# One PSUM ring, a paired fc2, and a new interleave of chunk and head in a spectral-network kernel

## The chip, the core and the metric

The kernel runs on one core of one Trainium2 chip. The metric is the device time of one launch in microseconds. Its engines are TensorE (PE, whose weight loads are the row PEld), VectorE (DVE), ScalarE (ACT), GpSimd (POOL) and SyncE (SP); POOL and SP do little else here than issue DMAs. Every engine works its own instructions in order and waits for the others by semaphores.

## The reference, cut to what matters

The input x is (8, 8, 256, 256), 8 images of 8 channels in 4 groups. Layer 0 is a Fourier network on the normalised x, added to x; layer 1 adds to that a 3x3 dilation (max) of its own normalised value.

```python
h = gconv1x1(concat([xg, grid]), fc0_w, fc0_b)      # 4 groups, width 10 each
for i in range(4):
    h = spectral_conv(h, sp_w1[i], sp_w2[i]) + gconv1x1(h, w_w[i], w_b[i])
    if i < 3:
        h = gswish(h, betas[i])
h = gswish(gconv1x1(h, fc1_w, fc1_b), betas[3])     # 128 hidden units per group
x = x + gconv1x1(h, fc2_w, fc2_b)                   # 2 channels per group
x = x + dilate3x3(group_norm(x))
```

`spectral_conv` keeps 24 x 12 modes of the 2-D Fourier transform, mixes the 10 channels of a group there with complex weights, and transforms back.

## The kernel before, in words

**Layers.** The state of one image lies in SBUF as `h`, 11 chunks of [128, 4, 512]. A layer begins with four stages that have no chunk loop. `spectrum_h` (L304 to L324) transposes and transforms along the rows, `mix` (L344 to L370) multiplies the modes with the weights `sw`: six pairs of a product and a sum of 800 elements on VectorE, then one fold on TensorE (L362) and copies into `fz`. `rows_of` (L380, L385, L395) goes back along the rows into `zt`. In the first layer `spectrum_x` takes the place of `spectrum_h`. Then `layer` goes over 11 chunks. For chunk c, `burst` (L432 or L435, then L438) makes two PSUM pairs `p_z`, and ScalarE (L444) writes `silu` of them into `h`; in the last layer VectorE (L446) and ScalarE (L448) write one pair each, and the chunk is stored to DRAM (`stored`, L450). `turn` (L407, copied by VectorE at L410) transposes the new chunk into a slot of `turned`, and `transform` (L420, copied at L421 into `zt`) makes the first transform of the next layer. The last layer has neither.

**Head.** fc1, its swish, and fc2 of an image form the *head*: 128 steps. `first(n)` makes four matmuls of 32 x 512 (L521), two groups into each of two PSUM pairs, and ScalarE (L524) writes `act` in two instructions of 128 x 1024. `second(n)` makes four matmuls (L537) from `act`. Sixteen steps accumulate into one PSUM tile `p_fc2`; then VectorE adds bias and x (L541), takes statistics (L542), and POOL stores the rows (L544). The head reads its state from DRAM, 1 MB per 12 steps into one of two tiles `hs` (L508, POOL's queue).

**Dilation.** `dilate` goes over 8 row blocks of an image: a DMA into `yin` (L561, POOL), six larger VectorE instructions (L572 to L586), and a DMA out (L587).

**Order.** PE, DVE and ACT keep the order in which the program issues (`manual_schedule`); POOL's and SP's DMAs are placed by the scheduler. The head of image b runs among the layers of image b + 1: each stage of the layers yields a cost (`CHUNK` = 1.25 for a chunk, 1 to 3 for other pieces), and 128 steps are spread over the sum of the costs. So image 0's layers run without a head, and image 7's head runs alone. Each step also advances the dilation of the image before by one of its 35 pieces. `unit` delays the second half of a unit (`second` of a step, `turn` of a chunk) behind the first half of the next one. So a chunk of the first three layers with one step stands on TensorE as: transform(c-2), burst(c), second(n-1), first(n), turn(c), transform(c-1), and so on.

**PSUM.** Eight banks: three pairs of the kind `z` (two banks each, used in rotation by `p_z`, `p_t`, `p_fc` of first and others), and two single banks `a` (`p_d`, `p_fc2` and others). A tile of a kind is given again when all its readers are done, in rotation; the first matmul into it waits for that.

```python
def ps_z(name):
    return ps.tile([128, 2, 512], F32, tag="z", bufs=3, name=name)
def ps_a(name):
    return ps.tile([128, 512], F32, tag="a", bufs=2, name=name)
```

Of the kernel before, what the change touches and what calls it, by code (L numbers as in the profile page):

```python
# [2 lines left out]

# [1 line left out]

# [16 lines left out]
G = 4  # L22
# [15 lines left out]
PIX = 2 * HW  # L38
DR = 2
STEPS = 128  # L40
CHUNK = 1.25


@with_exitstack
def fno_dilate_kernel(ctx: ExitStack, tc: tile.TileContext, a: dict, out: bass.AP):
# [6 lines left out]
    ps = ctx.enter_context(tc.tile_pool(name="ps", bufs=2, space=PSUM))  # L52
    dram = ctx.enter_context(tc.tile_pool(name="dram", bufs=2, space=bass.MemoryType.DRAM))

    def ps_z(name):
        return ps.tile([128, 2, 512], F32, tag="z", bufs=3, name=name)

    def ps_a(name):
        return ps.tile([128, 512], F32, tag="a", bufs=2, name=name)

    def part(i):
        return slice(32 * i, 32 * i + 32)
# [34 lines left out]
    h = const.tile([128, NCH, NQ, PIX], F32, tag="h", name="h")  # L97
    for c in range(NCH):
        nc.gpsimd.memset(h[:, c], 0.0)
    turned = const.tile([128, 4, 2048], F32, tag="turned", name="turned")  # L100
    yin = const.tile([128, DR + 2, HW + 2], F32, tag="yin", name="yin")
    nc.gpsimd.memset(yin, -BIG)
    y_rows = [dram.tile([C * HW + 2, HW], F32, tag=f"y{i}", bufs=1, name=f"y_rows{i}") for i in range(2)]
# [90 lines left out]
        out_["mr"] = mr  # L194

    late = [None]  # L200

    def unit(burst, after):
        burst()
        if late[0] is not None:
            late[0]()
        late[0] = after

    def flush():
        if late[0] is not None:
            late[0]()  # L210
        late[0] = None


    def spectrum_x(b, out_):

        x = turned[:, 0:2]
# [12 lines left out]
            nc.vector.tensor_scalar(x[:, i], x[:, i], mr[:, 0:1], mr[:, 1:2], ALU.subtract, ALU.mult)  # L229
        yield 1  # L230
        xt = turned[:, 2].rearrange("p (f r c) -> p f r c", f=2, r=8)
        a0 = turned[:, 3].rearrange("p (c r) -> p c r", c=128)
        for half in range(2):
            xn = x[:, half].rearrange("p (r w) -> p r w", r=8)
            for r in range(0, 8, 4):
# [101 lines left out]
    def mix(b, l, out_):  # L337

        s = [sb.tile([128, 3, G, 2, WID], F32, tag=f"S{i}", bufs=1, name=f"S{i}_{b}_{l}") for i in range(2)]
        bt, sw = out_["bt"], out_["sw"]  # L340
        for k in range(3):
            for k2 in range(2):
                pr = turned[:, 2 + k2, :800].rearrange("p (g m i) -> p g m i", g=G, i=WID)
                nc.vector.tensor_tensor(  # L344
                    pr, sw[k], bt[:, k2, k].unsqueeze(2).to_broadcast([128, G, 2 * WID, WID]), ALU.mult)
                nc.vector.tensor_reduce(  # L346
                    s[k2][:, k].rearrange("p g s o -> p (g s o)"),
                    pr.rearrange("p g m i -> p (g m) i"), AX.X, ALU.add,
                )
            if k == 0:  # L350
                sw.append(load_sw(l, 2))
            yield 3
        f = sb.tile([128, 2, 3, G, WID], F32, tag="F", bufs=1, name=f"F_{b}_{l}")
        nc.vector.tensor_tensor(f[:, 0], s[0][:, :, :, 0, :], s[1][:, :, :, 1, :], ALU.subtract)
        nc.vector.tensor_tensor(f[:, 1], s[0][:, :, :, 1, :], s[1][:, :, :, 0, :], ALU.add)
        yield 1

        p = ps_a(f"p_f_{b}_{l}")
        for slot in range(2):
            for n, (table, part_of) in enumerate(((0, slot), (1 + slot, 1 - slot))):  # L360
                for q in range(4):
                    mm(p[part(q), 120 * slot : 120 * slot + 120], fold[part(q), table, :],  # L362
                       f[part(q), part_of].rearrange("p k g o -> p (k g o)"), start=n == 0, stop=n == 1)
        nc.vector.tensor_copy(fz[0:32, :, :, 24], cz[:, l])
        if l < 2:
            nc.vector.tensor_copy(fz[0:32, :, :, 25], cz[:, 4 if l == 0 else 3])
        for q in range(4):
            dst = fz[part(q), :, :, 6 * q : 6 * q + 6].rearrange("p o g k -> p k g o")
            src = p[part(q), :240].rearrange("p (k g o) -> p k g o", g=G, o=WID)
            nc.vector.tensor_copy(dst, src)  # L370
        yield 2
# [27 lines left out]
    def layer(b, l, out_, stored, side):  # L399
        group_in_f = l % 2 == 1  # L400

        def turn(c):

            for v in range(2):
                t = ps_z(f"p_t_{b}_{l}_{c}_{v}")
                for i in range(8):
                    nc.tensor.transpose(  # L407
                        t[:, i // 4, 128 * (i % 4) : 128 * (i % 4 + 1)],
                        h[:, c, i // 2, 256 * (i % 2) + 128 * v : 256 * (i % 2) + 128 * (v + 1)], ident)
                nc.vector.tensor_copy(  # L410
                    turned[:, c % 4, 1024 * v : 1024 * (v + 1)], t.rearrange("p u w -> p (u w)"))

        def transform(c):

            t = turned[:, c % 4].rearrange("p (v f s q i) -> p v q f s i", v=2, q=NQ, f=NQ, s=2)
            p = ps_a(f"p_d_{b}_{l}_{c}")
            for v in range(2):
                for g in range(G):
# [30 lines left out]
            if l == 3:  # L449
                nc.sync.dma_start(stored[c], h[:, c].rearrange("p f w -> p (f w)"))  # L450

        def after(c):
            if l < 3:
                turn(c)

        def read_x(c):
            for g in range(G):
                nc.sync.dma_start(
# [6 lines left out]
        if l == 0:  # L465
            for c in range(NCH):
                read_x(c)
            norm_x(0)
            norm_x(1)
        for c in range(NCH):  # L470
            if l == 0 and c + 2 < NCH:
                norm_x(c + 2)
            if l < 3 and c > 1:
                transform(c - 2)
            unit(partial(burst, c), partial(after, c))
            next(side, None)
            yield CHUNK
        if l < 3:
            out_["sw"] = [load_sw(l + 1, 0), load_sw(l + 1, 1)]
            yield 1  # L480
            if late[0] is not None and late[0].func is after:
                flush()
            transform(NCH - 2)
            yield 2
            transform(NCH - 1)
# [8 lines left out]
    def layers(b, stored, d, then):  # L494


        for l in range(4):
            if l > 0:
                yield from spectrum_h(b, l, d)
# [3 lines left out]
        yield from then  # L503


    def load_state(b, c, stored):
        t = sb.tile([128, NQ, PIX], F32, tag="hs", name=f"hs_{b}_{c}")
        nc.gpsimd.dma_start(t.rearrange("p f w -> p (f w)"), stored[c])  # L508
        return t

    def head(b, stored, stats):
        hs = {0: load_state(b, 0, stored)}
        box = {}

        def first(n):

            c, blk, j = n // 12, n % 12 // 4, n % 4
            act = sb.tile([128, G, 512], F32, tag="act", name=f"act_{b}_{n}")
            pair = [ps_z(f"p_fc1_{b}_{n}_{i}") for i in range(2)]
            for g in range(G):  # L520
                mm(pair[g // 2][:, g % 2, :], w1[part(g), blk, :], hs[c][part(g), j, :],  # L521
                   start=True, stop=True)
            for i in range(2):
                nc.scalar.activation(act[:, 2 * i : 2 * i + 2, :], pair[i], AF.Silu)  # L524
            box[n] = act

        def second(n):

            t, rb = n // 16, n % 16
            if rb == 0:  # L530
                box["acc"] = ps_a(f"p_fc2_{b}_{t}")
                box["y"] = sb.tile([128, 512], F32, tag="yp", name=f"y_{b}_{t}")
                nc.gpsimd.dma_start(
                    box["y"], a["x"][b].rearrange("c (p t f) -> (c p) t f", p=16, t=8)[:, t])
            act, acc = box.pop(n), box["acc"]
            for g in range(G):
                mm(acc[part(g), :], w2[:, g, 15 - rb : 47 - rb], act[:, g, :],  # L537
                   start=rb == 0, stop=rb == 15)
            if rb == 15:
                y = box["y"]  # L540
                nc.vector.scalar_tensor_tensor(y, acc, b2, y, ALU.add, ALU.add)  # L541
                nc.vector.bn_stats(stats[:, t, :], y)  # L542
                whole = y_rows[b % 2][:]
                nc.gpsimd.dma_start(  # L544
                    bass.AP(whole.tensor, whole.offset + (1 + 2 * t) * HW, [[16 * HW, 128], [1, 512]]), y)

        for n in range(STEPS):
            if n % 12 == 0 and n // 12 + 1 < NCH:
                hs[n // 12 + 1] = load_state(b, n // 12 + 1, stored)
            unit(partial(first, n), partial(second, n))  # L550
            yield


    def dilate(b, stats):
# [33 lines left out]
            yield  # L588


    heads, tails = [], []

    def step():

# [2 lines left out]
        b, gen = heads[0]  # L597
        if next(gen, b) is b:
            heads.pop(0)
            flush()  # L600
            tails.append(dilate(b, stats_of.pop(b)))
            return step()
        if tails and next(tails[0], tails) is tails:
            tails.pop(0)
        return True

    stats_of = {}
    share, total = 0.0, None
    with tc.manual_schedule(engines={PE, DVE, ACT}):
        d = {}  # L610
        for _ in start(0, d):
            pass
        for b in range(n_img):
            stored = [dram.tile([128, NQ * PIX], F32, tag=f"hs{c}", name=f"stored_{b}_{c}") for c in range(NCH)]
            count, ahead = 0, {}
            for n in layers(b, stored, d, start(b + 1, ahead)):
                count += n
                if total is not None:
                    share += n * STEPS / total
                    while share >= 1.0:  # L620
                        share -= 1.0
                        step()
            total = total or count
            d = ahead
            if late[0] is not None and late[0].func.__name__ == "after":
                flush()
            stats_of[b] = sb.tile([128, 8, 6], F32, tag="bn_y", name=f"bn_y{b}")
            heads.append((b, head(b, stored, stats_of[b])))
        while step():
# [11 lines left out]
def _row_of():  # L641

    rows = np.full((NBLK, NQ, NCH, 2), -1)
    for n in range(HW // 2):
        c, blk, j = n // 12, n % 12 // 4, n % 4
        rows[blk, j, c] = 16 * (n % 16) + 2 * (n // 16) + np.arange(2)
    return rows

# [133 lines left out]
```

## Time and profile before

| | us |
|---|---|
| three runs | 4831.79, 4833.0, 4838.88 (median 4833.0) |
| profiled execution, its own time | 4834.64 |
| its span | 4832.9 |
| mean granted TensorE clock | 0.967 |
| PE busy | 4460.5 (92%) |
| ACT busy | 2640.7 (55%) |
| DVE busy | 2324.6 (48%) |
| POOL busy | 230.1 (5%) |
| DMA | 350.61 MB, 73 GB/s |

The profiled execution lies 1.6 us above the median of the runs, and its span 1.7 us below its own time. Busy time is the union of an engine's instructions. On TensorE several small matmuls run side by side in different rows or columns of the array, and their ends are modelled, so a busy PE can still be waiting: the distance between the starts of two groups of matmuls tells more. The bracket at the end of a line of the timeline gives the idle time before it and what ended that.

### The profile page before, as it was taken

What the parts mean: (1) busy time and instruction counts of PE and PEld (TensorE: products, weight loads), DVE (VectorE), ACT (ScalarE), POOL (GpSimd) and SP (SyncE); (2) the same over time, 40 slices, a digit from 0 to 9 for tenths busy, and PEclk for the clock granted to TensorE, in tenths of its full rate; (3) what the DMA queues carried; (4) which work ended last, traced back from release to release, by engine and by line L of the source; (5) the groups of instructions that cost most, each with busy time, mean ns of one, the idle gap of its engine ahead of it and who ended that gap; (6) DMA issues with size and microseconds to landing.
All of it is one profiled execution on the core that took longest, in us unless ns stands there. A gap on an engine that the chain in (4) does not pass through costs nothing.

```text
span 4832.9 us, 114725 instructions
## 1 busy us (share of the span) xinstructions
PE 4460.5 (92%) x52314; PEld 1956.3 (40%) x52314; DVE 2324.6 (48%) x3195; ACT 2640.7 (55%) x2717; POOL 230.1 (5%) x365
## 2 busy tenths in 40 slices
PE   4776999999999999999999999999899999999991
PEld 2443444434443444434444344433444344443220
DVE  6556443457434664446544474345643465442303
ACT  1221565655555656565555655565555565656881
POOL 2000000001000000000000000000100000000100
PEclk8998999999999999999999999999999999999996
DMA  2004010332104221141112421042210412113211
GB/s 69 12 12 164 21 47 33 123 103 79 35 35 163 65 73 38 60 151 58 55 46 84 135 72 36 33 143 83 88 33 30 163 62 72 38 40 142 99 51 55
DMA packets 73689, 350.61 MB, mean 73 GB/s; under 512 B 12600, under 2 KB 13620, under 8 KB 46516
## 3 DMA queue, kind: packets, MB, share of 16 engines
q0 software_dynamic: 37248, 176.18, 10.7%
q1 hardware_dynamic: 35955, 167.10, 10.2%
q8 instruction: 410, 6.72, 0.6%
q14 instruction: 76, 0.61, 0.0%
HBM read 217.40 MB, written 125.83 MB: 71 GB/s over the span
## 4 chain that ended last, share of the span: by engine, by line
PE 80%; issue 7%; DVE 7%; DMA 2%; ACT 1%; POOL 1%; POOLq 0%; DVEq 0%; ACTq 0%
PE p_fc L521 22%; PE p_fc L537 18%; PE p_t L407 11%; PE p_z L438 8%; PE p_z L435 7%; PE p_d L420 5%; PE p_z L432 2%; DMA yin<-y_rows 2%; PE p_g L380 2%; DVE turned L410 2%; PE p_g L385 1%; PE p_b L317 1%; PE p_at L304 1%; PE p_a L250 1%; DVE fz L370 1%
## 5 line engine op out<-in xcount | busy, mean ns | idle before, releaser
L524 ACT ACTIVATE act<-p_fc 128x1024 f32<-128x1024 f32 x2048 | 1984.6, 1022 | 907.7 <-PE p_fc L521 881.9
L521 PE MATMUL p_fc<-hs,c_w 32*128 32x512 f32 x8192 | 1347.7, 645 | 15.0 <-ACT act L524 13.8
L410 DVE COPY turned<-p_t 128x1024 f32<-128x1024 f32 x528 | 625.1, 1220 | 1007.1 <-PE p_t L407 1006.2
L537 PE MATMUL p_fc<-act,c_w 128*32 128x512 f32 x8192 | 1103.0, 610 | 0.2 <-ACT act L524 0.2
L444 ACT ACTIVATE h<-p_z 128x1024 f32<-128x1024 f32 x528 | 511.7, 1021 | 913.4 <-PE p_z L438 866.2
L521 PEld LDWEIGHTS p_fc<-hs,c_w 32*128 32x128 f32 x8192 | 459.8, 185 | 694.7 <-issue 374.2
L407 PE MATMUL p_t<-ident,h 128*128 128x128 f32 x4224 | 573.8, 281 | 5.5 <-ACT act L524 1.2
L407 PEld LDWEIGHTS p_t<-ident,h 128*128 128x128 f32 x4224 | 456.2, 141 | 248.6 <-ACT h L444 183.2
L537 PEld LDWEIGHTS p_fc<-act,c_w 128*32 128x32 f32 x8192 | 162.7, 108 | 652.6 <-issue 639.2
L438 PE MATMUL p_z<-c_binv,zt 32*128 32x256 f32 x5632 | 409.2, 405 | 0.1
L435 PE MATMUL p_z<-h,c_wt 32*32 32x512 f32 x8448 | 371.0, 605 | 14.2 <-DVE turned L252 5.3
L438 PEld LDWEIGHTS p_z<-c_binv,zt 32*128 32x128 f32 x5632 | 257.6, 186 | 306.5 <-issue 295.0
L420 PE MATMUL p_d<-turned,c_fw 128*32 128x240 f32 x4224 | 272.7, 371 | 20.9 <-DVE turned L410 19.0
L395 DVE COPY zt<-p_g 128x264 f32<-128x264 f32 x320 | 168.4, 609 | 179.8 <-PE p_g L380 89.8
L446 DVE TENSOR_SCALAR h<-p_z,c_bias 128x1024 f32<-128x1024 f32 x88 | 113.0, 1284 | 286.7 <-PE p_z L438 286.7
L448 ACT ACTIVATE h<-p_z,c_bias 128x1024 f32<-128x1024 f32 x88 | 98.0, 1114 | 185.3 <-PE p_z L438 185.3
L344 DVE TENSOR_TENSOR turned<-t,B 128x800 f32<-128x800 f32 x192 | 188.8, 983 | 15.0 <-DMA t<-in_spw 14.7
L346 DVE TENSOR_REDUCE S<-turned 128x80 f32<-128x800 f32 x192 | 189.3, 986 | 6.6
L541 DVE SCALAR_TENSOR_TENSOR y<-p_fc,c_b,y 128x512 f32<-128x512 f32 x64 | 48.0, 750 | 281.7 <-PE p_fc L537 281.5
L420 PEld LDWEIGHTS p_d<-turned,c_fw 128*32 128x32 f32 x4224 | 113.5, 109 | 141.8 <-issue 63.5
L421 DVE COPY zt<-p_d 128x240 f32<-128x240 f32 x264 | 106.0, 401 | 125.3 <-PE p_d L420 125.3
L508 POOL DMA_DIRECT2D hs<-stored x88 | 47.0, 535 | 2438.8 <-PE p_fc L521 1998.9
(127 smaller groups left out, 2351.5 us busy)
## 6 DMA issues: line engine op xcount, KB each, us to landing
stored<-h SPq DMA_DIRECT2D x88, 1024.0 KB
hs<-stored POOLq DMA_DIRECT2D x88, 1024.0 KB, 5.1
t<-in_spw SPq DMA_DIRECT2D x96, 400.0 KB
yin<-y_rows POOLq DMA_DIRECT2D x64, 512.0 KB, 4.7
h<-in_xp SPq DMA_DIRECT2D x352, 48.0 KB
turned<-in_x SPq DMA_DIRECT2D x16, 1024.0 KB
y<-in_x POOLq DMA_DIRECT2D x64, 256.0 KB, 3.0
y_rows<-y POOLq DMA_DIRECT2D x64, 256.0 KB, 2.6
```

What stands on the lines that cost most here:

```text
L344: nc.vector.tensor_tensor(pr, sw[k], bt[:, k2, k].unsqueeze(2).to_broadcast([128, G, 2 * WID, WID]), ALU.mult)
L346: nc.vector.tensor_reduce(s[k2][:, k].rearrange("p g s o -> p (g s o)"), pr.rearrange("p g m i -> p (g m) i"), AX.X, ALU.add,)
L395: nc.vector.tensor_copy(dst, src)
L407: nc.tensor.transpose(t[:, i // 4, 128 * (i % 4) : 128 * (i % 4 + 1)], h[:, c, i // 2, 256 * (i % 2) + 128 * v : 256 * (i % 2) + 128 * (v ...
L410: nc.vector.tensor_copy(turned[:, c % 4, 1024 * v : 1024 * (v + 1)], t.rearrange("p u w -> p (u w)"))
L420: mm(p[part(g), :240], fw[:, v, :], m[:, :, :, : NBLK * WID], start=v == 0, stop=v == 1)
L435: mm(o, wt[part(q), l, g, :], h[part(q), c, f, :], start=True, stop=False)
L438: mm(pair[q // 2][:, q % 2, HW * s : HW * (s + 1)], zt[part(q), 2 * c + s].rearrange("p f o -> p (f o)"), binv[part(q), :], start=False, s ...
L444: nc.scalar.activation(dst, pair[i], AF.Silu)
L521: mm(pair[g // 2][:, g % 2, :], w1[part(g), blk, :], hs[c][part(g), j, :], start=True, stop=True)
L524: nc.scalar.activation(act[:, 2 * i : 2 * i + 2, :], pair[i], AF.Silu)
L537: mm(acc[part(g), :], w2[:, g, 15 - rb : 47 - rb], act[:, g, :], start=rb == 0, stop=rb == 15)
```

## The change

PSUM has now one kind: four pairs `z`. `ps_a` takes one half of a pair, and the next `ps_a` gets the other half if no `ps_z` was called between.

`second(n)` is called for every second step only, before `first(n+3)`. It makes fc2 of steps n and n+1 into one half pair, and VectorE adds it to `y` in SBUF: 64 additions per image instead of 8 (8 of them with the bias). `act` has four buffers instead of two.

`unit` and the delayed halves are gone. A chunk stands as burst(c), turn(c-1), transform(c-2), and then the head steps that its cost asks for: 2, 2, 1, 1 after successive chunks (17 per layer), in the last layer 1, 2 (16). The rest of the 128 steps, 61, is spread over the other stages. A step more is put in ahead of the chunks where the count of steps is odd.

The head's state comes in pieces of 256 KB (`hs`, [128, 512], four buffers, two ahead), 44 per image, each for three steps; the steps go over the chunks four times. `turned` has three slots instead of four. The dilation is advanced at every third step (`TAIL`).

```diff
-CHUNK = 1.25
+CHUNK = (2, 2, 1, 1)
+LAST = (1, 2)
+TAIL = 3
...
+    spare = [None]
     def ps_z(name):
-        return ps.tile([128, 2, 512], F32, tag="z", bufs=3, name=name)
+        spare[0] = None
+        return ps.tile([128, 2, 512], F32, tag="z", bufs=4, name=name)
     def ps_a(name):
-        return ps.tile([128, 512], F32, tag="a", bufs=2, name=name)
+        if spare[0] is not None:
+            t, spare[0] = spare[0], None
+            return t[:, 1, :]
+        t = ps_z(name)
+        spare[0] = t
+        return t[:, 0, :]
...
-    turned = const.tile([128, 4, 2048], F32, tag="turned", name="turned")
+    turned = const.tile([128, 3, 2048], F32, tag="turned", name="turned")
...
-    def unit(burst, after):
-        burst()
-        if late[0] is not None:
-            late[0]()
-        late[0] = after
...
+        yield ()
         for c in range(NCH):
             if l == 0 and c + 2 < NCH:
                 norm_x(c + 2)
+            burst(c)
+            if l < 3 and c > 0:
+                turn(c - 1)
             if l < 3 and c > 1:
                 transform(c - 2)
-            unit(partial(burst, c), partial(after, c))
             next(side, None)
-            yield CHUNK
+            yield (CHUNK[c % len(CHUNK)] if l < 3 else LAST[c % len(LAST)],)
...
         def second(n):
             t, rb = n // 16, n % 16
             if rb == 0:
...
-            act, acc = box.pop(n), box["acc"]
-            for g in range(G):
-                mm(acc[part(g), :], w2[:, g, 15 - rb : 47 - rb], act[:, g, :],
-                   start=rb == 0, stop=rb == 15)
-            if rb == 15:
-                y = box["y"]
+            y, acc = box["y"], ps_a(f"p_fc2_{b}_{n}")
+            for i in range(2):
+                act = acts.pop(n + i)
+                for g in range(G):
+                    mm(acc[part(g), :], w2[:, g, 15 - rb - i : 47 - rb - i], act[:, g, :],
+                       start=i == 0, stop=i == 1)
+            if rb == 0:
                 nc.vector.scalar_tensor_tensor(y, acc, b2, y, ALU.add, ALU.add)
+            else:
+                nc.vector.tensor_tensor(y, acc, y, ALU.add)
+            if rb == 14:
                 nc.vector.bn_stats(stats[:, t, :], y)
...
         for n in range(STEPS):
-            if n % 12 == 0 and n // 12 + 1 < NCH:
-                hs[n // 12 + 1] = load_state(b, n // 12 + 1, stored)
-            unit(partial(first, n), partial(second, n))
+            if n % 32 % NBLK == 0:
+                load_state(n // 32 * NCH + n % 32 // NBLK + 2)
+            if n % 2 == 1 and n > 2:
+                second(n - 3)
+            first(n)
             yield
+        second(STEPS - 2)
...
-        if tails and next(tails[0], tails) is tails:
+        count[0] += 1
+        if tails and count[0] % TAIL == 0 and next(tails[0], tails) is tails:
             tails.pop(0)
```

## The prediction

> **What bounds the kernel now.** I read the busy table first, then the stretches, then the timeline inside each stretch. Of the page:
>
> ```profile
> PE 4460.5 (92%) x52314; PEld 1956.3 (40%) x52314; DVE 2324.6 (48%) x3195; ACT 2640.7 (55%) x2717; POOL 230.1 (5%) x365
> ...
> L541 DVE SCALAR_TENSOR_TENSOR y<-p_fc,c_b,y 128x512 f32<-128x512 f32 x64 | 48.0, 750 | 281.7 <-PE p_fc L537 281.5
> ```
>
> TensorE is busy nearly always; the others are half idle. The windows cut the run into image 0's layers, the seven stretches in which a head runs among layers, the last head alone, and the last dilation:
>
> ```profile
> 75.00:475.00 400.00, 293.61 (x4494) 172.91 (x4498) 234.08 (x308) 80.30 (x81) 1.07 (x2) 0.88 0.17 60
> 475.00:4444.00 3969.00, 3861.60 (x45602) 1696.11 (x45598) 1931.47 (x2637) 2300.02 (x2364) 168.83 (x282) 0.99 0.22 74
> 4444.00:4732.00 288.00, 285.29 (x2076) 76.22 (x2068) 56.63 (x90) 253.13 (x263) 23.80 (x41) 1.00 0.21 73
> ```
>
> Columns: length, busy PE, PEld, DVE, ACT, POOL, granted clock (0.99 where it matters), DMA share, GB/s. Busy PE hides waiting, so I take starts from the timeline. Where steps of the head stand alone:
>
> ```profile
> 2457.04 1.37 PE L521 MATMUL p_fc<-hs,c_w 32*128 32x512 f32 x8
> ...
> 2458.34 1.07 PE L537 MATMUL p_fc<-act,c_w 128*32 128x512 f32 x8
> ...
> 2459.34 1.14 PE L521 MATMUL p_fc<-hs,c_w 32*128 32x512 f32 x8
> ...
> 2460.41 0.16 PEld L537 LDWEIGHTS p_fc<-act,c_w 128*32 128x32 f32 x8 [0.76 <-issue]
> ...
> 2460.57 1.94 ACT L524 ACTIVATE act<-p_fc 128x1024 f32<-128x1024 f32 x2 [0.36 <-PE p_fc L521]
> ```
>
> fc1 to fc2 takes 1.30 in one step and 1.07 in the next, fc2 to fc1 1.00: 4.37 us for two steps where 4.13 would do, and ScalarE idles 0.36 in the same two steps. Three pairs for two steps of two pairs each: fc1's second pair waits for ScalarE. In image 2's stretch (2290 to 2861, 570.5 us) I took the distance of starts between all neighbouring groups, and of each kind the smallest that recurs as its unhindered cost. That sum is 516.5; so 54 us are waiting: 16.6 in fc1 before fc2; 12.9 in the last layer (second pair of L435 or L521); 5.7 in fc1 before turn (33 times 0.17); 6.0 before one fold L362; 5.5 before L385; 7.3 elsewhere. One fold, and image 0's chunk without a head:
>
> ```profile
> 2323.29 1.82 PE L362 MATMUL p_f<-F,c_fold 32*32 32x120 f32 x32 [5.88 <-DVE F L354]
> ```
>
> ```profile
> 225.20 2.34 PE L407 MATMUL p_t<-ident,h 128*128 128x128 f32 x16
> ...
> 226.34 2.47 DVE L410 COPY turned<-p_t 128x1024 f32<-128x1024 f32 x2 [2.75 <-PE p_t L407]
> ...
> 228.86 0.61 PE L420 MATMUL p_d<-turned,c_fw 128*32 128x240 f32 x8 [0.63 <-DVE turned L410]
> ```
>
> The fold waits for mix on VectorE, which has two dilation blocks of 3.9 us in its queue there. In image 0, turn takes 2.41 (second pair waits) and transform 1.79 (waits for the copies), where 2.09 and 0.95 recur elsewhere: 6.36 us a chunk where 5.20 would do.
>
> **Same work in another order (per image with a head).** The number of matmuls stays. fc2 costs 0.995 before an fc1 and 0.88 before a group of its own form (L420, L385). Before: 105 x 0.995 + 23 x 0.88 = 124.7 us. After: 64 doubles. fc2 before fc2 does not occur here; by L420 it is 0.88, at most 0.995. 64 x (0.88 + 0.995) = 120.0, so -4.7. Twenty fc1 stand before an fc1: passes after the first of one form follow at 0.43 per 512 columns (L438: 0.216 per 256), so 0.96; bounds 0.86 and 1.07. 20 x 0.11 = 2.2. fc1 straight before L432 or L435 will stand 40 times; here it never takes under 1.26, but with its second pair waiting, so I take 1.07; 1.26 would cost 7.6. Sum **-6.9** (bounds +4 and -9).
>
> **The waits that go.** All 54 are waits for a pair or for VectorE. In a chunk with two steps the allocations are Z Z T T D A A F B B. With four pairs, each waits for the one four places back: T for ScalarE's reading of fc1, done 1 us before; F for the copy of T, done 0.6 us before. turn(c-1) and transform(c-2) wait for nothing recent. So the chunk runs unhindered unless VectorE is late.
>
> **The waits that come.** VectorE gets 56 more instructions per image of 128x512 from PSUM: between 0.69 (L586, from SBUF) and 0.75 (L541); I take 0.72, the form lying between. 40 us per image beside 276 (1931.5 / 7) of 567: hidden on average, not in mix. There VectorE needs 0.76 (L324) + 6 x 1.92 (L344 and L346, start to start) + 0.5 = 12.8 us, plus the additions queued between, plus a dilation block where one falls. TensorE has fewer head steps to cover it, since 17 go to a layer's chunks where 11 or 12 went: in the built order, from L317 to the fold, 7, 7, 6 and 7 fc1 with 3, 4, 3 and 4 doubles (before: 9 steps of 2.07 = 18.6):
>
> - layer 1: 12.8 + 3 x 0.72 + 3.9 = 18.9 against 12.8 on TensorE: 6.1 waited
> - layer 2: 15.0 against 14.7: 0.3
> - layer 3: 15.0 against 11.8, and 3.9 more if a dilation block falls there: 3.2 to 7.1, I take 5.2
> - layer 0: 16.0 (L276, L283, L286 for L324) + 4 x 0.72 = 18.9 against 14.7: 4.2
>
> Sum 15.8. The additions also make TensorE feel this earlier, since their pairs are in the ring; that is the same wait, not another. After two of the folds only one fc1 covers the copies into `fz` (2.33): 2.0. L304 follows the last transform at once: 1.5. Eight first halves of dilation (3.9 us, now also among chunks, ahead of copies on whose pairs TensorE waits some 3 us later): 1 each, 8. Last layer: the pair that VectorE empties (1.28) is wanted after an fc1 (1.07): 3. Head steps elsewhere: 3. Sum **33.3**. No row shows these waits; bounds: 12 (mix's surplus nearly alone) and 70 (more than all of today's).
>
> [...]
>
> **DMA.** The state now comes in 352 loads instead of 88, each issued by POOL in 0.54 us (L508); POOL is 5% busy. A load of 256 KB lands in 3.0 us (y), 1 MB in 5.1. Four buffers give six or more steps (12 us) of lead, and POOL's queue holds behind it only stores whose VectorE result is as old. Cost 0; without that cover 3.0 per load, 44 per image. Now y is wanted at the first of 16 steps, not the last; its load stands in POOL's built order right after the store of two tiles before, 16 steps ahead: 0. Three slots of `turned`: the slot is read three chunks before: 0.
>
> **The sum.** Per image -6.9 - 54 + 33.3 = -27.6; seven times **-193**. Image 0: 33 x 1.16 = 38 and 5 in its last layer (3.67 a chunk, two pairs in hand); loads may hold layer 0, so **-40** (bounds -15, -50). Head alone: a double step of 1.07 + 0.88 + 1.00 + 1.07 = 4.02; by the ring, fc1's second pair of the odd step waits for ScalarE's first of the even one, some 0.1, so 4.13 instead of 4.365: 64 x 0.235 = 15, and one wait of 0.7 for `hs` goes: **-16** (bounds 0, -25). The last dilation keeps its 101 us. 4834.6 - 249 = 4585.6 for the profiled execution, which lay 1.6 above the median: **4584**.
>
> **Rivals.**
> - *The ring hides nearly all.* Waits of 15 per image: -6.9 - 54 + 15 = -46; 7 x 46 + 56 = 378, so 4455. For it: VectorE idles half its time. Against: mix's chain alone is longer than its cover. Chance 0.22.
> - *VectorE takes the gain.* Waits of 52: -9 per image; 63 + 56 = 119, so 4714. For it: the 5.88 above, and every mix now has a quarter less cover. Chance 0.20.
> - *Slower: in-order VectorE paces the whole ring.* 64 additions and 33 copies of `p_d` per image now sit in the ring that fc1 uses. If each makes TensorE wait w, waits are 33.3 + 97 w; the gain of 27.6 x 7 + 56 is used up at w = 0.37. With w = 0.72, one more instruction queued ahead: 97 x 0.72 = 70 per image, +42; 7 x 42 - 56 = 238, so 5071. For it: VectorE has waits for TensorE 1006 us long in L410 alone, in order. Against: those are idle, not late. Chance 0.09.
> - *It does not do what it says:* steps wait as before, because ScalarE and not pairs sets the pace: 4833. Against: ScalarE's two instructions start 0.92 apart, 3.7 for two steps. Chance 0.03.
>
> **How the numbers follow.** Forecast 0.46, about 4584 (4510 to 4650). The range 4430 to 4760 leaves out the lower part of the first rival (0.06), the upper of the second (0.05), and the last two. About 0.2% is what a measurement of this kernel can tell from no change. Faster 0.88, same 0.03, slower 0.09.
>
> **What would show it.** Right: two lone steps at 4.0 to 4.2; no 0.17 in fc1 before turn; image 0's layers some 40 us shorter; the largest waits of TensorE before L362's fold, for VectorE. Wrong: waits of fc1 for the additions throughout; waits for `hs`; VectorE waiting for y; fc2 before fc2 at over 1.0.

## The result, and the profile after

| | before | changed kernel |
|---|---|---|
| median of the runs, us | 4833.3 | 4852.3 (4851.6 to 4855.0) |
| profiled span, us | 4832.9 | 4849.8 |
| mean granted clock | 0.967 | 0.957 |
| end of image 0 (its last fold), us | 474.7 | 427.5 |
| from there, mean of six images, us each | 568.5 | 581.2 |
| from the last of these folds to the end, us | 947.0 | 935.2 |

The ratio is 1.0038 (95% interval 1.0021 to 1.0056): slower by some 0.4%, where 5% faster was forecast. Image 0 gained 47 us (forecast 40). The last row holds three things: the layers of image 7, with a head among them, up to the first fc1 of the last head (563.1 to 561.7 us, forecast 27.6 less), that head alone (283.2 to 273.9, forecast 16 less), and the last dilation (100.8 to 99.6). So the miss lies in the images with a head: six are 12.7 us longer each and the seventh is 1.4 shorter, where 27.6 less was forecast for each.

The page of the changed kernel, part 1 and two groups of part 5 (busy, mean ns | idle time just before, and its releaser):

```profile
PE 4309.0 (89%) x52314; PEld 1968.3 (41%) x52314; DVE 2603.7 (54%) x3643; ACT 2616.4 (54%) x2717; POOL 374.4 (8%) x629
...
L536 DVE TENSOR_TENSOR y<-p_fc,y 128x512 f32<-128x512 f32 x343 | 236.2, 689 | 490.2 <-PE p_fc L531 489.3
...
L531 PE MATMUL p_d<-act,c_w 128*32 128x512 f32 x1456 | 177.6, 606 | 87.3 <-DVE zt L415 87.3
```

TensorE is busy 152 us less and yet ends later, so it waits more. The additions take 0.69 each, where the forecast took 0.72. The last line is the find: fc2 (L531) writes into a tile with the name `p_d`, the transform's, and waited 87.3 us for `p_d`'s copy. (1456 matmuls in 16s are 91 double steps: 13 in each of seven images.)

The windows of the changed kernel, with the columns as before (length, busy PE, PEld, DVE, ACT, POOL, clock, DMA share, GB/s):

```profile
75.00:427.00 352.00, 269.09 (x4486) 172.49 (x4486) 229.00 (x305) 80.32 (x81) 2.63 (x4) 0.88 0.19 65
427.00:4465.00 4038.00, 3753.25 (x45554) 1709.05 (x45558) 2178.14 (x3032) 2276.25 (x2358) 294.39 (x512) 0.97 0.23 73
```

In the middle stretch the granted clock is 0.97 where it was 0.99. A chunk of image 0, in the timeline:

```profile
216.21 1.97 PE L401 MATMUL p_t<-ident,h 128*128 128x128 f32 x16
...
218.10 1.02 PE L414 MATMUL p_d<-turned,c_fw 128*32 128x240 f32 x16
219.05 1.16 PE L429 MATMUL p_z<-h,c_wt 32*32 32x512 f32 x32
...
220.13 1.15 PE L432 MATMUL p_z<-c_binv,zt 32*128 32x256 f32 x16
221.21 1.97 PE L401 MATMUL p_t<-ident,h 128*128 128x128 f32 x16
```

No bracket at all: turn to turn is 5.00 us, where it was 6.36 and 5.20 was forecast. Without a head the ring does what it was to do. The head alone:

```profile
4601.28 2.00 PE L516 MATMUL p_fc<-hs,c_w 32*128 32x512 f32 x16
...
4603.59 1.97 PE L531 MATMUL p_fc<-act,c_w 128*32 128x512 f32 x16 [0.31 <-ACT act L518]
...
4605.49 2.00 PE L516 MATMUL p_fc<-hs,c_w 32*128 32x512 f32 x16
```

Two steps take 4.21 (before 4.37, forecast 4.13): fc2's pair is the fourth after fc1's first, which ScalarE is still reading; that costs 0.28 us. (The forecast had 0.1, in the second pair of fc1.) Where head and chunks run together, it goes otherwise:

```profile
2400.29 1.02 PE L414 MATMUL p_d<-turned,c_fw 128*32 128x240 f32 x16
...
2401.80 0.40 DVE L415 COPY zt<-p_d 128x240 f32<-128x240 f32 x1
2402.25 0.16 PEld L531 LDWEIGHTS p_d<-act,c_w 128*32 128x32 f32 x8 [1.40 <-DVE zt L415]
2402.25 1.92 PE L531 MATMUL p_d<-act,c_w 128*32 128x512 f32 x16 [0.94 <-DVE zt L415]
```

fc2 has nothing to do with `p_d`; it has only been given the other half of the same pair, and TensorE waits 0.94 us for the reader of `p_d` all the same. Transform to fc2 takes 1.96 us here; transform to fc1 takes 0.95. And before a fold in layer 2:

```profile
2313.15 2.65 PE L516 MATMUL p_fc<-hs,c_w 32*128 32x512 f32 x16
...
2313.94 0.68 DVE L536 TENSOR_TENSOR y<-p_fc,y 128x512 f32<-128x512 f32 x1
...
2314.53 1.22 DVE L573 TENSOR_TENSOR m<-yin 128x1024 f32<-128x1024 f32 x1
...
2314.67 0.30 PEld L516 LDWEIGHTS p_fc<-hs,c_w 32*128 32x128 f32 x4 [0.37 <-DVE y L536]
...
2318.38 0.28 DVE L348 TENSOR_TENSOR F<-S,S 128x120 f32<-128x120 f32 x1
...
2318.80 1.82 PE L356 MATMUL p_f<-F,c_fold 32*32 32x120 f32 x32 [3.00 <-DVE F L348]
...
2323.00 3.21 PE L531 MATMUL p_f<-act,c_w 128*32 128x512 f32 x16 [2.37 <-DVE fz L364]
```

Three things in these lines. Two fc1 take 2.65 us (2.00 where nothing waits): the addition (L536), queued on VectorE behind mix, holds the pair that is fourth back, and the last weight loads of fc1 wait for it. A dilation block (L573 and three more, 3.9 us) stands in VectorE's queue ahead of `F`, so the fold starts 3.00 us late. Then fc2 shares the fold's pair and waits 2.37 for the copies into `fz`.

I summed the distances between starts for five images (from the second of these folds to the seventh) as the forecast had done for one, with the smallest recurring distance of each kind as its unhindered cost. Per image:

| | before | forecast | changed kernel |
|---|---|---|---|
| unhindered sum | 510.5 | -6.9 | 503.7 (-6.8) |
| waits in the chunks | 33.8 | 14 | 42.4 |
| waits in mix, up to the fold | 11.7 | 15.8 | 23.0 |
| fold to the next burst | 12.4 | 2.0 | 14.8 |
| spectra | 2.9 | 1.5 | 1.3 |
| all waits | 60.8 | 33.3 | 81.5 |

### The profile page after: what moved, and what is told of

Same layout as the page of the kernel before. It is cut to its first block, busy times and chain, and to the rows that moved or that the text cites. A ratio compares the mean times of both kernels' runs of the same rounds, so it can differ in the third digit from the quotient of the medians.

```text
span 4849.8 us, 116052 instructions
## 1 busy us (share of the span) xinstructions
PE 4309.0 (89%) x52314; PEld 1968.3 (41%) x52314; DVE 2603.7 (54%) x3643; ACT 2616.4 (54%) x2717; POOL 374.4 (8%) x629
## 4 chain that ended last, share of the span: by engine, by line
PE 73%; DVE 19%; ACT 4%; issue 3%; DMA 1%; POOL 0%; SPq 0%; POOLq 0%; ACTq 0%; DVEq 0%
PE p_fc L516 16%; PE p_fc L531 13%; PE p_t L401 9%; PE p_z L432 8%; PE p_z L429 6%; DVE turned L404 4%; PE p_d L531 4%; PE p_d L414 3%; ACT act L518 3%; PE p_z L426 3%; DVE S L340 3%; DVE turned L338 3%; PE p_b L311 2%; PE p_g L379 2%; PE p_g L374 2%
## 5 line engine op out<-in xcount | busy, mean ns | idle before, releaser
L516 PE MATMUL p_fc<-hs,c_w 32*128 32x512 f32 x8192 | 1226.9, 636 | 49.8 <-DVE y L536 43.4
L531 PE MATMUL p_fc<-act,c_w 128*32 128x512 f32 x6400 | 799.7, 615 | 33.2 <-ACT act L518 22.2
L516 PEld LDWEIGHTS p_fc<-hs,c_w 32*128 32x128 f32 x8192 | 395.0, 185 | 730.1 <-issue 485.4
L401 PE MATMUL p_t<-ident,h 128*128 128x128 f32 x4224 | 540.5, 283 | 1.7 <-ACT act L518 1.7
L401 PEld LDWEIGHTS p_t<-ident,h 128*128 128x128 f32 x4224 | 477.6, 145 | 102.8 <-ACT act L518 76.5
L536 DVE TENSOR_TENSOR y<-p_fc,y 128x512 f32<-128x512 f32 x343 | 236.2, 689 | 490.2 <-PE p_fc L531 489.3
L508 POOL DMA_DIRECT2D hs<-stored x352 | 198.1, 563 | 3108.0 <-PE p_fc L516 2602.5
L531 PEld LDWEIGHTS p_fc<-act,c_w 128*32 128x32 f32 x6400 | 178.2, 111 | 530.7 <-issue 300.8
L429 PE MATMUL p_z<-h,c_wt 32*32 32x512 f32 x8448 | 332.1, 599 | 17.3 <-DVE h L440 8.3
L531 PE MATMUL p_d<-act,c_w 128*32 128x512 f32 x1456 | 177.6, 606 | 87.3 <-DVE zt L415 87.3
L338 DVE TENSOR_TENSOR turned<-t,B 128x800 f32<-128x800 f32 x192 | 188.6, 982 | 0.4 <-DMA t<-in_spw 0.2
L429 PEld LDWEIGHTS p_z<-h,c_wt 32*32 32x32 f32 x8448 | 74.9, 103 | 216.8 <-ACT act L518 88.8
L426 PE MATMUL p_z<-h,wc 6*32 6x512 f32 x2816 | 147.8, 617 | 14.8 <-ACT act L518 10.4
```

What stands on the lines that cost most here:

```text
L338: nc.vector.tensor_tensor(pr, sw[k], bt[:, k2, k].unsqueeze(2).to_broadcast([128, G, 2 * WID, WID]), ALU.mult)
L401: nc.tensor.transpose(t[:, i // 4, 128 * (i % 4) : 128 * (i % 4 + 1)], h[:, c, i // 2, 256 * (i % 2) + 128 * v : 256 * (i % 2) + 128 * (v ...
L426: mm(o, wc[k, :], h[k, c, f, :], start=True, stop=False)
L429: mm(o, wt[part(q), l, g, :], h[part(q), c, f, :], start=True, stop=False)
L516: mm(pair[g // 2][:, g % 2, :], w1[part(g), blk, :], hs[k][part(g), :], start=True, stop=True)
L531: mm(acc[part(g), :], w2[:, g, 15 - rb - i : 47 - rb - i], act[:, g, :], start=i == 0, stop=i == 1)
```

## The experiments

**Theory:** the shared pair, the additions in mix and the dilation in mix each cost TensorE 10 us or more per image. **Rivals:** the ring is short of pairs wherever it is used, so that a wait taken away comes back at the next tile; or in-order VectorE paces the ring everywhere, and all three are one wait. Medians are of four or five runs; each ratio is to runs of the kernel before on the same chip, made in the same session. The medians of those are 4833 for e1 to e4, 4839 for e5 to e8, 4838 for e9, e10 and b1, and 4836 for e12, so a difference of some 5 us between two such sets says nothing.

| run | us | ratio to before, 95% interval |
|---|---|---|
| e1_own_pair | 4737.0 | 0.9795 (0.9780 to 0.9810) |
| e2_no_additions | 4745.1 | 0.9816 (0.9802 to 0.9829) |
| e3_one_per_chunk | 4810.2 | 0.9950 (0.9938 to 0.9963) |
| e4_three_pairs | 5282.8 | 1.0927 (1.0912 to 1.0942) |
| e5_own_one | 4706.5 | 0.9723 (0.9705 to 0.9740) |
| e6_own_no_dilation_in_mix | 4661.7 | 0.9635 (0.9622 to 0.9648) |
| e7_own_tail1 | 4763.6 | 0.9846 (0.9833 to 0.9860) |
| e8_own_no_additions | 4621.0 | 0.9554 (0.9541 to 0.9568) |
| e9_split_mix | 4650.7 | 0.9614 (0.9601 to 0.9627) |
| e10_split_one | 4621.5 | 0.9546 (0.9530 to 0.9561) |
| b1_before_no_dilation_in_mix | 4771.7 | 0.9864 (0.9851 to 0.9878) |
| e12_all_own | 4600.6 | 0.9512 (0.9499 to 0.9525) |

**1. A pair of its own for `p_d`.**

```diff
-            p = ps_a(f"p_d_{b}_{l}_{c}")
+            p = ps_z(f"p_d_{b}_{l}_{c}")[:, 0, :]
```

> The transform's p_d takes a pair of its own, so that fc2 never stands in the other half of it. Theory (the shared pair): in the trace of the changed kernel transform to fc2 takes 1.96 us where transform to fc1 takes 0.95, 13 times per image, because fc2 waits for VectorE's copy of p_d out of the same pair; without it 7 x 13 x 1.0 = some 92 us go, and the kernel takes 4740 to 4790. Rival (the ring is short of pairs, or VectorE paces it): a pair more is taken per chunk, the same wait shows up as fc1 waiting for a pair, and the time stays within 20 us of 4852.

Measured 4737.0: 115 us less, 3 below the theory's range. The same place in its timeline:

```profile
2312.62 1.02 PE L414 MATMUL p_d<-turned,c_fw 128*32 128x240 f32 x16
...
2313.45 1.90 PE L531 MATMUL p_fc<-act,c_w 128*32 128x512 f32 x16
...
2314.12 0.40 DVE L415 COPY zt<-p_d 128x240 f32<-128x240 f32 x1
```

fc2 now starts before the copy, 0.84 after transform. The waits in the chunks fall from 42.4 to 26.7 per image, 15.7 where the theory counted 13, and those in mix stay (22.9): nothing came back at the next tile. The theory holds; the rival of a ring short of pairs falls.

**2. The additions left out, with the shared pair and without it.** Both leave out

```diff
-            else:
-                nc.vector.tensor_tensor(y, acc, y, ALU.add)
```

> Leaves out part of the work: the 56 additions per image of fc2's results into y (all but the first of each tile), so each of these pairs is free when TensorE has written it. Theory (additions cost only where VectorE is behind in mix): of the waits, those of fc1 for y (some 20 us per image) shrink and the waits before the folds lose 3 to 4 x 0.7 us each; 10 to 25 us per image, 4680 to 4780. Rival (in-order VectorE paces the whole ring): nearly all of the 70 us of waiting per image goes, under 4450. Third: additions cost nothing, 4852 within 15.

> Leaves out the same 56 additions per image as before, now with the own pair for p_d. Theory (shared pair and additions are separate costs): 4737 less 107, some 4630, at least 60 less. Rival (both measure the same wait on in-order VectorE): over 4700.

Measured: 107 us less than the changed kernel, and 116 less than with the own pair. The two costs stand side by side. The additions cost TensorE 15 to 17 us per image, 0.27 to 0.30 us for each of the 56: less than the 0.37 from which the forecast's slower rival would have eaten the whole gain. Against e1, e8 waits 12 us less per image in mix, 3 less between fold and burst, and 3 elsewhere. So the additions cost where VectorE is behind, not throughout.

**3. The dilation kept out of mix,** with the own pair. `mix` yields its costs as negative numbers, and

```diff
-        if tails and count[0] % TAIL == 0 and next(tails[0], tails) is tails:
+        if late:
+            count[1] += 1
+        if late and tails and count[1] % TAIL == 0 and next(tails[0], tails) is tails:
...
-                    step()
+                    step(isinstance(n, tuple) or n > 0)
```

with `TAIL` 2 in place of 3.

> Own pair for p_d, and a dilation takes no step while mix runs (and every second step of the head elsewhere, so that it still ends in time). Theory (a dilation block of 3.9 us in VectorE's queue makes the fold late): with every third step carrying one, some 1.75 blocks per image stood in a mix, with the shorter halves 8 us per image, and the granted clock gains a little: 4640 to 4690. Rival (the additions, not the dilation, make mix late): 4725 to 4745.

Measured 4661.7: 75 less. In 24 mixes of six images the own-pair kernel had 7 blocks, 1.2 per image and not 1.75; here there is none. The fold of layer 1, in its timeline:

```profile
2371.04 0.68 DVE L536 TENSOR_TENSOR y<-p_fc,y 128x512 f32<-128x512 f32 x1
...
2371.64 0.27 DVE L348 TENSOR_TENSOR F<-S,S 128x120 f32<-128x120 f32 x1
...
2375.75 1.02 PE L356 MATMUL p_f<-F,c_fold 32*32 32x120 f32 x32
```

`F` follows the addition at once, starts 4 us ahead of the fold, and the fold takes 1.02 us instead of 1.82. Against the own pair, the waits in mix fall from 22.9 to 16.3 us per image and those from the fold to the burst from 14.4 to 10.6: 10.4 of the 12.9 us by which these five images became shorter. First product (L338) to fold became 1.3 us shorter per mix (17.2 to 15.9). The granted clock rose from 0.958 to 0.969, and the part from the last steady fold to the end fell from 916.8 to 912.2 us; what the clock alone gave was not taken apart.

**4. The dilation at every step again,** with the own pair: `TAIL` 1.

> Own pair for p_d, and the dilation takes a step with every step of the head, as in the kernel before, in place of every third. Theory (where it is put decides, not how it is spread): as many blocks stand in a mix, together in one of them instead of spread over four: within 25 us of 4737. Rival (the spreading costs, since it touches every mix): 4680 to 4710. Other rival (the spreading is worth something): over 4765.

Measured 4763.6: 27 more, at the edge of the theory's 25, and the ratios differ by 0.5%, which is 25 us; the total does not decide. The trace does: the six images are equal (564.2 and 564.7 us), as the theory has it, and the difference is in the part from the last steady fold to the end (947 and 917 us), above all where the head runs alone beside a dilation (296.8 and 272.3):

```profile
4424.69 1.99 PE L516 MATMUL p_fc<-hs,c_w 32*128 32x512 f32 x12
...
4427.99 0.68 DVE L536 TENSOR_TENSOR y<-p_fc,y 128x512 f32<-128x512 f32 x1
...
4428.73 1.13 PE L516 MATMUL p_fc<-hs,c_w 32*128 32x512 f32 x4 [2.05 <-DVE y L536]
...
4429.79 3.25 PE L531 MATMUL p_fc<-act,c_w 128*32 128x512 f32 x16
```

With every step a piece, both halves of a block stand ahead of an addition, and fc1 waits 2.05 us for its pair. I had looked only at mix for this part of the change.

**5. More cover for mix:** one step per chunk, first with the shared pair, then with the own pair.

```diff
-CHUNK = (2, 2, 1, 1)
-LAST = (1, 2)
+CHUNK = (1,)
+LAST = (1,)
```

> CHUNK and LAST are (1,), so one step of the head goes with each chunk (44 per image in place of 65) and the steps left over go to mix, the spectra and the rows (84 in place of 62). Theory (mix on VectorE is longer than its cover, and the granted clock falls with the waiting there: 0.96 to 0.97 per image where the kernel before had 0.99): the cover of each fold grows by about a third, 5 us, and with the clock some 20 to 30 us per image go; 4650 to 4720. Rival (mix is not what costs; the waits sit among the chunks): within 30 us of 4852.

> Own pair for p_d, and one step of the head per chunk (44 per image in place of 65, the other 84 outside the chunks). Theory (waiting in mix for want of cover): without the shared pair, which one step per chunk meets more often (16 times per image in place of 13), the gain of the cover adds to that of the own pair: 4737 less some 55, 4670 to 4700. Rival (the two overlap, the gain of one step per chunk is not from mix): 4720 to 4750.

(The counts named there are off by two and one: the changed kernel has 67 steps with the chunks and 61 outside them.) Measured 42 less than the changed kernel, where the theory had 132 to 202, and 31 less than with the own pair, where it had some 55: the right sign both times, but neither the theory's range nor the rival's was met. With one step per chunk fc2 follows transform 16 times per image and layer 0's waits shrink, but the further double steps in mix bring their additions into VectorE's queue: fc1 to fc2 waits 21 us per image in e5 and 15.5 in e1. In mix, cover and load come together.

**6. Mix let in the head more often, and `p_b` unshared,** on top of experiment 3.

```diff
-        p = ps_a(f"p_b_{b}_{l}")
+        p = ps_z(f"p_b_{b}_{l}")[:, 0, :]
...
+                if k2 == 0:
+                    yield -1.5
...
-            yield -3
+            yield -1.5
```

> No dilation in mix and own pair for p_d, and two things more: mix lets the head in after each of its six pairs of VectorE instructions instead of after every second (so an addition stands behind at most 1.9 us of mix and not 3.8), and p_b has a pair of its own too (fc2 waited 0.88 us for its copies, three times per image). Theory (fc1 waits for an addition that is queued behind mix, and the pair it holds is the fourth back): half of some 7 us of these waits per image and 2.6 for p_b go: 4662 less 30 to 50, 4610 to 4630. Rival (the sum of VectorE's work in mix sets the fold, the waits only move there): within 15 of 4662.

> As the one with mix split, and one step of the head per chunk (84 in place of 62 outside the chunks). Theory (cover of mix is still short): as much as one step per chunk gave with the own pair, 30 less: 4580 to 4600. Rival (with no dilation in mix and the additions let in sooner the cover suffices): the same time as the kernel with mix split, within 10.

Measured 4650.7, 11 less than experiment 3, and so within the rival's 15. By the distances the waits moved: 3.8 us per image less in mix (16.3 to 12.5), but 2.0 more from the fold to the burst and 2.2 more in the chunks. (What `p_b` did in it was not tried by itself.) With one step per chunk on top, 4621.5: 29 less, the size expected; it ends above its range because the step before it gave 11 and not 30 to 50. More cover of mix is a part of that only: the waits fall by 2.4 us per image in mix and 5.1 in the chunks, and rise by 5.7 in the spectra.

**7. The ring taken away:** three pairs and two single banks, as before, with all else as changed.

```diff
     def ps_z(name):
-        spare[0] = None
-        return ps.tile([128, 2, 512], F32, tag="z", bufs=4, name=name)
+        return ps.tile([128, 2, 512], F32, tag="z", bufs=3, name=name)
...
+        return ps.tile([128, 512], F32, tag="a", bufs=2, name=name)
```

> The changed kernel with the PSUM of the kernel before: three pairs in a ring and two single banks for p_d, fc2 and the small tiles, all else as changed. Theory (the ring of four gains in the chunks but loses by the shared pair): transform to fc2 falls to 0.95 (92 us less in all), and each chunk with two steps waits for a third pair again, 0.3 to 0.4 us in each of 33 chunks, and lone steps by 0.1; together 4790 to 4860. Rival (the ring is the whole gain of the change): image 0 grows by 40 us again and every image by 30, over 5000.

Measured 5282.8: my theory misses by over 420 us, and even the rival was too kind to it. The new order needs the fourth pair, since it sets two fc1 in a row. Its head alone:

```profile
5120.99 1.92 PE L525 MATMUL p_fc<-act,c_w 128*32 128x512 f32 x16
...
5122.84 1.99 PE L510 MATMUL p_fc<-hs,c_w 32*128 32x512 f32 x12
...
5125.15 1.13 PE L510 MATMUL p_fc<-hs,c_w 32*128 32x512 f32 x4 [0.33 <-ACT act L512]
5126.21 0.16 PEld L525 LDWEIGHTS p_fc<-act,c_w 128*32 128x32 f32 x8 [0.76 <-issue]
```

(fc1 is L510 here, fc2 L525.) The last four matmuls of the second fc1 start 2.31 us after the first group, since their pair is the third back; a double step takes 5.22 us in place of 4.21. In the chunks L423 to L426, the two halves of burst, takes 2.31 in place of 1.11: 37 us of waiting per image. So the ring is worth 430 us to this order, and the two parts can't be judged one by one. One part of the theory did come: with a single bank for `p_d` and another for fc2, transform to fc2 takes 0.84.

**8. The same cure for the kernel before:** its dilation kept out of mix, by the edit of experiment 3.

> The kernel before, with its dilation kept out of mix and nothing else. Theory (the block of 3.9 us in mix costs whichever order is used, and less where fewer additions are queued with it): before folds and the rows after them the kernel before waits 6.8 and 5.1 us per image, of which most goes: 4750 to 4790. Rival (only the changed kernel is short of cover in mix): 4820 to 4840.

Measured 4771.7, 1.4% faster than it was: the theory. Part of what helps the changed kernel is no merit of the change.

**9. All together:** as e10, and `p_f` with `ps_z` too.

> As the kernel with mix split and one step per chunk, and the fold's p_f has a pair of its own too. Theory (the shared pair costs wherever fc2 follows a small tile: fold to fc2 takes 3.4 us and more in place of 0.95, once per image): 7 x 2.5 = 17 us less, 4600 to 4610. Rival (the rows wait for the same copies right behind, so nothing is won): within 8 of 4621.

Measured 4600.6: 21 less, as expected. This version is 4.9% faster than the kernel before (interval 4.75 to 5.0) and close to the 4584 that the change alone was given; one step per chunk, whole pairs for `p_d`, `p_b` and `p_f`, no dilation in mix and the head let into mix more often make the difference. Of its page:

```profile
PE 4233.3 (92%) x52314; PEld 1970.3 (43%) x52314; DVE 2612.7 (57%) x3643; ACT 2616.7 (57%) x2717; POOL 373.8 (8%) x629
```

VectorE's work is the changed kernel's (2603.7); only its place in the order is another, and TensorE is at 92% again.

## Why the prediction was wrong, by its own steps

- **The same work in another order, -6.9:** -6.8 measured. fc1 before a burst stands at 1.07 and fc1 before fc1 at 0.962, as taken; a double fc2 takes 1.85 (forecast 1.875).
- **The waits that go, 54 and no less: the step that failed.** The prediction wrote one order down, "In a chunk with two steps the allocations are Z Z T T D A A F B B", and concluded "So the chunk runs unhindered unless VectorE is late". But `second` is called ahead of `first(n)` when n is odd. So that order holds where the chunk's first step is even. Where it is odd, fc2's tile (F) follows transform's (D) directly. Both are half tiles, and between them no `ps_z` is called: F is the other half of D's pair, and fc2 waits for a copy issued a moment ago. The trace shows this 13 times per image: 3 in layer 1 and 2 in layer 2, mostly at the second of two one-step chunks, and 8 in layer 0, where the two-step chunks begin with an odd step too. (The step put ahead of the chunks makes the count even, but it is taken off the first chunk's two, and the count is odd again.)
- **What it cost.** By the distances 13.7 us per image; taking it away gave 115 us, 16.4 per image. That is the largest single item of the 268 us by which the forecast missed, and less than half of them. With the own pair alone (4737.0) the time lies within the wide range that was given (4430 to 4760), but not within 4510 to 4650.
- The same step took ScalarE to be done with a pair "1 us before". In layer 0 the odd order sets two fc1 straight ahead of a burst (D F A A B B Z Z), and there it isn't:

```profile
2219.66 2.01 PE L516 MATMUL p_fc<-hs,c_w 32*128 32x512 f32 x16
...
2220.90 3.77 ACT L518 ACTIVATE act<-p_fc 128x1024 f32<-128x1024 f32 x4 [4.69 <-PE p_fc L516]
2221.97 2.05 PE L426 MATMUL p_z<-h,wc 6*32 6x512 f32 x32 [0.30 <-ACT act L518]
```

  TensorE makes two fc1 in 2 us and ScalarE reads them in 3.8; burst takes 1.98 to its second half instead of 1.1. That and the wait ahead of it are some 8 us per image. With one step per chunk the first of the two fell from 6.1 to 2.1 us (e1 to e5).
- **The waits that come, 33.3:** 81.5 in all were measured. Of the 48 more, 28 are in the chunks, half of it the shared pair, and the 8 of layer 0 are in it too. Mix was given 15.8 and took 23.0. The additions were counted nearly rightly (3 ahead of each `F`; 3 or 4 forecast), the dilation blocks too (1.2 per image; the sum held one and a part). The additions' price in mix was a little low: with the own pair, leaving them out took 12 us per image from mix, where the sum had 10, and some 6 more elsewhere, where it had none. The wait does not stand where the forecast looked for it: of the 22.9 in mix with the own pair, 5.5 stand before the fold and 12.9 between fc1 and fc2, of which 3.2 are left without the additions. The copies behind the fold were given 2.0; fold to burst waits 14.8, of which 3.3 are fc2 in the fold's own pair and 5.1 the first rows (L374) waiting for the copies into `fz` behind one fc1. But this stretch had 12.4 before, so it was the gain of 10 there that did not come.
- **`turned` with three slots, the DMAs in smaller pieces: 0.** No wait of TensorE for `hs` and none of VectorE for the loads of y shows: right.
- **Image 0, -40:** -47. **The head alone, -16:** -9; the double step takes 4.21 for 4.13. **The last dilation:** the span ends 99.6 us after the last fc2 starts, before 100.8: unchanged, as taken.
- **The signs it named.** Of the right ones, the 0.17 in fc1 before turn is gone and image 0 is shorter; two lone steps miss the bound of 4.2 by 0.01. That TensorE's largest waits stand before the fold did not come: the longest are 3.65 us in the first rows (L374) for the copies into `fz`, 3.45 in fc2 for the copy of `p_d` and 3.39 in fc1 for an addition, and the folds follow with 3.00. In total fc2 behind `p_d` leads with 87.3 us. Of the wrong signs fc1's waits for additions came, but in mix and not throughout. None of the signs looked at transform followed by fc2.
- **The rivals.** "VectorE takes the gain" named the additions and mix rightly, but these are not enough by themselves. The pacing rival had the sign right. By its formula, 33.3 + 97 w, the measured waits would give w = 0.50; but an addition costs 0.27 to 0.30, two thirds of it in mix, and the copies of `p_d` hold up fc2 by a shared pair, not fc1 by the ring. That the time is so near to "It does not do what it says" (4833) is chance: over the span, +76 in six images, -47 in image 0 and -12 in the end make +17. No rival held the shared pair, and without one for "two tiles are one" the range could not hold the time.

## What to carry to other kernels

Before counting how far back a ring's tile was last used, write down the allocations in the order in which the code issues them, for each parity of every counter and from the count that the loop really starts with, and look for two that share a tile: here fc2 waited 87.3 us in all for the reader of the other half. When results move from PSUM accumulation to additions on VectorE, price them stage by stage: here two thirds of their cost (12 of 18 us per image) fell in mix, where VectorE already sets the end, and it showed as waits for the pairs that the additions held. And keep work that nobody waits for, such as the dilation, out of that stage: it was worth 75 us here, with the own pair, and 66 to the kernel before.

## What the runs showed of the hardware

**The clock fell beside waits, and the work behind them took longer; in layer 0 it fell without one.** In the last fence of the first section the fold waits 3.00 us, then takes 1.82 where it takes 1.02 without a wait, and fc2 3.21 where it takes 1.92. The windows around it (PEclk is the third number from the end):

```profile
2304.00:2316.00 12.00, 11.36 (x80) 3.51 (x72) 11.79 (x15) 9.16 (x10) 1.07 (x2) 1.00 0.44 129
2316.00:2328.00 12.00, 6.83 (x112) 3.13 (x115) 5.88 (x12) 2.78 (x4) 0.37 (x1) 0.72 0.07 19
```

Between 430 and 4400 us the granted clock is 0.5 in stretches: of the changed kernel's 44, 30 are 3.41 us long, 9 twice and 5 three times that. They cost 61 us of full clock in the kernel before, 107 in the changed one, 97 with the own pair and 41 with no dilation in mix. How much of the time that is by itself was not tried. Of the 44 stretches of the changed kernel, 17 (34 of the 107 us) start in layer 0's chunks with no idle time of 0.6 us or more between matmuls in the 5 us before; of the 19 in the kernel before, none does. One starts at 2213.0:

```profile
2209.65 2.07 PE L426 MATMUL p_z<-h,wc 6*32 6x512 f32 x32
...
2212.72 3.45 PE L401 MATMUL p_t<-ident,h 128*128 128x128 f32 x16
```

Turn (L401) takes 3.45 us, where it took 1.97 in image 0 above. All 17 have a burst of layer 0 (L426) in the 6 us before. Why the clock falls there stays open, and so does what length of wait goes with it elsewhere: in experiment 4 the fc2 behind a wait of 2.05 us between matmuls (2.88 between weight loads) takes 3.25 us, and the clock of 4400 to 4500 us is 0.93 where it is 1.00 with the own pair.

**The wait on the shared pair goes with the tile.** `p_d` and fc2 lie in different halves of one pair, and the trace shows 1.40 us of weight-load idle ahead of fc2 for the copy of `p_d`; the own pair shows none. A whole pair is not needed for that: in experiment 7 `p_d` and fc2 have single banks of their own, and fc2 starts 0.84 us after transform there too. A ring of four pairs with a tile per half was not tried.
